# Another form of seven products, another choice of engines in the planner, and norms scaled two token tiles at a time

## The chip, the core and the metric

The kernel runs on one core of a Trainium2 chip. The metric is device time in microseconds (us) of one execution. The engines are TensorE (PE; PEld is its loading of weights), VectorE (DVE), ScalarE (ACT), GpSimd (POOL) and SyncE (SP), which issues every DMA here. All data are float32.

## What is computed

`x` is (64, 256, 128): 64 graphs of 256 nodes with 128 features; all share one adjacency matrix `adj` (256, 256). Four layers follow one another, each `x = layernorm(x + f(x))` over the 128 features.

- Layer 0, five steps of a gated unit. With `m = adj @ h`: `u3 = h @ u3_w.T`; `z = sigmoid([m, m] @ w3_w.T + u3)`; `r = sigmoid([m, m] @ w4_w.T + u3)`; `hv = tanh([m, m] @ w5_w.T + (r * h) @ u5_w.T)`; `h = (1 - z) * h + z * hv`, with biases.
- Layer 1: `h0 = x @ W[0]`, `h1 = x @ W[1]`, `A = softmax` of a masked edge vector; `diag(A) * h0 + offdiag(A) @ h1 + bias`.
- Layer 2: attention over the graph (`softmax` of leaky sums of two scores, masked by `adj`), a layer norm and relu, an aggregation with `adj`, a product with `W1`, a norm and relu, a product with `W2`, relu.
- Layer 3: `adj` is applied up to three times and every power has its own 128 x 128 weight; the sum of these products.

## The kernel before, in words

The 64 graphs are handled as 32 pairs. A pair's `x` is one tile of 128 partitions by 512 columns: four token tiles of 128 features each (two graphs by two halves of the nodes). Matmul operands and results are 512 columns too, so a result fills one PSUM bank; there are eight banks.

**The planner.** The program does not issue operations as it goes through the layers. Every operation is added to a `Schedule` (L119) with its possible engines and a duration for each (`ways`), and what it reads and writes. `order` (L150) then goes through the operations that are ready and always takes the one with the best key: the time at which it could start (plus, where there is a choice of engines, its duration and `SPARE`), and then how late its pair is (`DUE` us from pair to pair, `LAST_DUE` for the last `LAST` pairs, less the work that remains in the pair, plus `HOLD` of its layer). So 32 pairs in different layers are mixed. The order found is written out as it stands; each engine takes its own instructions in that order, and semaphores keep data right. `MARGIN` stretches the planned durations of all engines but PE, `LAG` and `SEEN` are the planned delay until another engine sees a result. `USES` (L44) says that POOL's operations and those of the class "DVE+" (DVE, operands in SBUF alone) exclude each other on a shared resource called PORT. `CLASSES` (L40) gives the number of tiles of each class: X for `x`, T for the transposed input, A for everything of 512 columns, B for 1024, H for layer 2's projected rows, PS for PSUM banks. An operation whose tile class has no free tile is not ready.

**Spreading over the graph.** `spread` (L533) computes `adj @ h` of a pair with four matmuls of 256 columns. `spread7` (L544) does the same with seven products of 128 columns in place of eight, in the manner of Strassen and Winograd: sums of blocks of `h` are made first (`add`, L557, on DVE or POOL), products go to four 128-column blocks X, Y, V, Z of one bank, and results are put together from them by `plus` (L566, DVE) and `copy` (L569 on ACT, L570 on DVE). Four differences of blocks of `adj` are made once (L464). `layer0` (L671) takes `spread7` for pairs from `FIRST` to `n_pairs - FINAL - 1`, else `spread` and an evacuation (`to_sbuf`, L497; `evacuate`, L229, on ACT at L231 or on DVE at L232). A float32 matmul stands in the trace as two instructions.

**Turning.** `turn` (L505) transposes the four 128 x 128 blocks of a tile. For most pairs that is a DVE transpose of 32 x 32 blocks (L520), one DMA to DRAM (L522) and four DMAs back (L528); for the last pairs (`BY_DMA` of them, for each place) it is PE transposes (L514) and an evacuation.

**Norms.** `stats` (L590) and `scale_stats` (L627) find a variance per token; POOL computes its power of -0.5 (L607, L651). `normalize` (L612) then does four token tiles on ACT (L620) or DVE (L615). `scale_tokens` (L654) scales by the token's factor: on ACT one instruction per token tile (L662), on DVE one for all (L664). Layer 1 and layer 2 call it for four token tiles by `scale_norm`, layer 3 for two token tiles of each of two banks.

In the first microseconds four warm-up matmuls run on a constant (L291), `adj`, the first two `x` and the weights arrive, and DVE prepares derived weights. The end is layer 3 of the last pairs (products L822, L823 and L830, statistics, scaling and the store of the result, L836).

Of the kernel before, what the change touches and what calls it, by code (L numbers as in the profile page):

```python
# [8 lines left out]
AF = mybir.ActivationFunctionType  # L9
ALU = mybir.AluOpType  # L10
AX = mybir.AxisListType

P = 128
N = 256
D = 128
STEPS = 5

BY_DMA = {"h": 0, "y": 2, "x1": 3, "x2": 2, "w": 3, "z": 1, "x3": 2}

WARM = 4  # L20


FAST = (0, 1, 2, 3, 4)
FIRST, FINAL = 0, 3

TURN, TT = 0.44, 0.61
LN_EPS = 1e-5
# [9 lines left out]
ROWS = ["l1_bias", "bp", "b1", "gat_g", "gat_b", "b2"]  # L37


CLASSES = {"X": (512, 15), "T": (512, 3), "A": (512, 34), "H": (520, 4), "B": (1024, 6), "S": (32, 64), "PS": (512, 8), "D": (512, 4), "E": (1024, 8)}  # L40

SEEN = {"PE": 0.23, "ACT": 0.16, "DVE": 0.16, "POOL": 0.12, "SP": 0.0}

USES = {"DVE+": ("DVE", "PORT"), "POOL": ("POOL", "PORT")}  # L44

AGAIN = {"DVE": 0.12, "POOL": 0.12}

SPARE = {"DVE": 0.0, "DVE+": 0.0, "POOL": 0.0}


DUE, LAST_DUE, LAST = 20.0, 9.0, 8

MARGIN, LAG = 1.03, 0.8

HOLD = (0.0, -20.0, 0.0, 80.0)


def mm(cols):
# [35 lines left out]
class Op:  # L94
    def __init__(self, pair, ways, reads, writes, number, dma):
        self.pair, self.ways, self.reads, self.writes, self.number, self.dma = pair, ways, reads, writes, number, dma
        self.seen = LAG + (sum(dma) if dma else SEEN[ways[0][0].rstrip("+")])
        self.before, self.then, self.waits, self.ready, self.rest = {}, [], 0, 0.0, 0.0


class Schedule:
# [29 lines left out]
    def order(self, tiles):  # L131
# [6 lines left out]
        for op in reversed(self.ops):  # L138
            us = min(w[1] for w in op.ways) + op.seen
# [6 lines left out]
        while ready:  # L146
            best = None
            for op in ready:
                held = 0.0
                for v in op.holds:  # L150
                    if v.cls and v.ap is None:
                        held = max(held, min((t for t, a in free[v.cls] if full.get(id(a)) or not v.seeded), default=1e9))
                if held == 1e9:
                    continue
                for engine, us, fn in op.ways:
                    us = us if engine == "PE" else us * MARGIN
                    start = max(op.ready, held, *(engines[e] for e in USES.get(engine, (engine,))))
                    late = self.due(op.pair) - op.rest + HOLD[op.layer] if op.pair >= 0 else -1e4
                    key = (start + (us + SPARE.get(engine, 0.0) if len(op.ways) > 1 else 0.0), late, op.number)
                    if best is None or key < best[0]:  # L160
                        best = key, start, op, engine, us, fn
            if best is None:
                raise RuntimeError("no operation can start: too few tiles")
            _, start, op, engine, us, fn = best
# [6 lines left out]
            end = start + us  # L171
# [11 lines left out]
                    full[id(v.ap)] = v.full or v.seeded  # L183
            for x in op.then:
                x.waits -= 1
                same = engine != "SP" and x.ways[0][0].rstrip("+") == engine.rstrip("+")
                x.ready = max(x.ready, end + (AGAIN.get(engine.rstrip("+"), 0.0) if same else op.seen))
                if not x.waits:
                    ready.append(x)

# [7 lines left out]
def kernel(ctx: ExitStack, tc: tile.TileContext, x, xT, adj, adjT, mats, cols, rows, out):  # L198
    nc = tc.nc
# [5 lines left out]
    S = Schedule(n_pairs)  # L205
# [10 lines left out]
    def dve(us, fn, r, w):  # L216
        S.add([("DVE", us, fn)], r, w)
# [18 lines left out]
    aT, a = fixed([2, N], "aT"), fixed([2, N], "a")  # L236
# [224 lines left out]

    aTt = fixed([4, P], "aTt")
    blk_a = lambda j, i: aT.ap[:, j, i * P:(i + 1) * P]
    for k, (p_, q_) in enumerate(((lambda: blk_a(0, 1), lambda: blk_a(0, 0)), (lambda: blk_a(1, 1), lambda: aTt.ap[:, 0, :]),  # L464
                                  (lambda: blk_a(1, 1), lambda: blk_a(0, 1)), (lambda: blk_a(1, 0), lambda: aTt.ap[:, 1, :]))):
        dve(0.25, lambda k=k, p_=p_, q_=q_: nc.vector.tensor_sub(aTt.ap[:, k, :], p_(), q_()), [aT, aTt], [aTt])
    centre(vx, lambda: vx.ap, 2)
    centre(vq, lambda: vq.ap, 2)

# [1 line left out]
    def bank():  # L471

        t = Value("PS", name="ps")
        t.full = True
        return t
# [18 lines left out]
    def tokens(v):  # L494
        return v.at(4, D)
# [48 lines left out]
    def spread7(h, right, terms):  # L544


        sv, t, o = Value("A", name="sums"), bank(), Value("A", name="mT")
        p1, p2, p3, p4 = (Part(sv) for _ in range(4))
        X, Y, Z, V = (Part(t) for _ in range(4))
        o1, o2, o3 = (Part(o) for _ in range(3))  # L550
# [4 lines left out]
        s1, s2, s3, s4 = (lambda k=k: blk(sv, k) for k in range(4))  # L555

        def add(o, x, y, op, r, w):  # L557
            fn = lambda e: e.tensor_tensor(o(), x(), y(), op=op)  # L558
            S.add([("DVE+", 0.2, lambda: fn(nc.vector)), ("POOL", 0.42, lambda: fn(nc.gpsimd))], r, w)

        def product(k, left, rt, r, w, start=False):
            pe(mm(128), lambda: nc.tensor.matmul(blk(t, k), left(), rt(), start=start, stop=True, skip_group_check=True),  # L562
               [*r, right, terms], w)

        def plus(to, k, other, r, w, n=1):
            dve(0.065 + 0.135 * n, lambda: nc.vector.tensor_add(to(), t.at(4, P)[:, k:k + n, :], other()), r, w)  # L566

        def copy(to, k, r, w):
            S.add([("ACT", 0.18, lambda: nc.scalar.copy(to(), blk(t, k))),  # L569
                   ("DVE", 0.2, lambda: nc.vector.tensor_copy(to(), blk(t, k)))], r, w)  # L570
# [12 lines left out]
        plus(lambda: blk(sv, 0), 2, lambda: blk(sv, 1), [V, p2], [p1])  # L583
        product(2, s4, B(1, 1), [p4, V], [V])
        plus(lambda: blk(o, 3), 3, lambda: blk(sv, 0), [Z, p1, o3], [o])
        product(3, H(1, 1), T(3), [h, Z], [Z])
        plus(lambda: o.at(4, P)[:, 1:3, :], 2, lambda: blk(sv, 1)[:, None, :].to_broadcast([P, 2, P]), [V, Z, p2], [o], 2)
        return o

    def stats(y, eps=None):  # L590
# [19 lines left out]
        return s, rs, nmr  # L610

    def normalize(y, o, s, rs, nmr):  # L612
        def by_dve():
            for c in range(4):
                nc.vector.tensor_scalar(tokens(o)[:, c, :], tokens(y)[:, c, :], rs()[:, c:c + 1], nmr()[:, c:c + 1],  # L615
                                        op0=ALU.mult, op1=ALU.add)

        def by_act():
            for c in range(4):
                nc.scalar.activation(tokens(o)[:, c, :], tokens(y)[:, c, :], AF.Identity, bias=nmr()[:, c:c + 1],  # L620
                                     scale=rs()[:, c:c + 1])
# [32 lines left out]
    def scale_tokens(v, o, tiles, s, rs):  # L654

        n, step = len(tiles), tiles[1] - tiles[0]
        ot = lambda: tokens(o)[:, tiles[0]::step, :]
        by = lambda: rs()[:, tiles[0]::step].unsqueeze(2).to_broadcast([P, n, D])

        def by_act():  # L660
            for k, c in enumerate(tiles):
                nc.scalar.mul(tokens(o)[:, c, :], v.at(n, D)[:, k, :], rs()[:, c:c + 1])  # L662
        ways = [("ACT", 0.315 * n, by_act),
                ("DVE" if v.cls == "PS" else "DVE+", 0.135 * n + 0.07, lambda: nc.vector.tensor_mul(ot(), v.at(n, D), by()))]  # L664
        if v.cls != "PS":
            ways.append(("POOL", 0.3 * n + 0.07, lambda: nc.gpsimd.tensor_mul(ot(), v.at(n, D), by())))
# [230 lines left out]
```

## Time and profile before

| what | value |
|---|---|
| median of three runs | 1525.11 us (1524.67 to 1527.51) |
| the profiled execution, its own time | 1524.61 us |
| its span, first to last instruction | 1522.8 us |
| granted TensorE clock | 0.999 |
| PE, PEld busy | 1502.2, 1063.2 us |
| DVE busy | 1296.3 us |
| ACT busy | 936.2 us |
| POOL busy | 562.4 us |
| DMA | 213.86 MB, mean 140 GB/s |

The page of the profile gives busy time by engine, the chain of work that ended last, and groups of instructions with the mean duration of one. Answers of the trace give the same by stage, by line and by who waited for whom. A line is that of the source; where a helper records operations, its line stands for many places, for example L566 for all additions of `spread7`. A busy PE is not a PE at its peak: matmuls are pipelined, so the spacing of their starts says more than their lengths.

### The profile page before, as it was taken

How to read it: one execution, taken by the hardware profiler on the slowest of the kernel's cores; microseconds unless marked ns; L12 is line 12 of the kernel's file. 1: busy time of each engine (PE TensorE's matmuls, PEld its weight loads, DVE VectorE, ACT ScalarE, POOL GpSimd, SP SyncE). 2: the span in 40 equal slices, each digit the busy share in tenths (PEclk: the TensorE clock that was granted, in tenths of full speed). 3: DMA queues.
4: the chain of work that ended last, by engine and by line, in shares of the span. 5: the costliest groups of instructions: out<-in, count | busy, mean ns of one | idle time of the engine just before them, and what ended most of it. 6: DMA issues, size and time to landing. Idle time of an engine off the chain costs nothing.

```text
span 1522.8 us, 26241 instructions
## 1 busy us (share of the span) xinstructions
PE 1502.2 (99%) x7190; PEld 1063.2 (70%) x7190; DVE 1296.3 (85%) x3443; ACT 936.2 (61%) x2805; POOL 562.4 (37%) x784
## 2 busy tenths in 40 slices
PE   9999999999999999999999999999999999999998
PEld 6565656666666677677666776766767666788997
DVE  8988888888989898888998888899888788889763
ACT  2444445666776666656757567677657566768763
POOL 4322223243435433433443344334434132245542
PEclk9999999999999999999999999999999999999999
DMA  7544456576868788686696796767975877776441
GB/s 220 113 97 82 93 117 125 125 159 122 170 132 164 155 169 171 136 164 137 140 177 128 162 185 138 152 134 173 167 147 128 169 133 153 149 149 139 106 89 49
DMA packets 933874, 213.86 MB, mean 140 GB/s; under 512 B 715616, under 2 KB 929248, under 8 KB 933728
## 3 DMA queue, kind: packets, MB, share of 16 engines
q1 hardware_dynamic: 933728, 212.19, 68.6%
q8 instruction: 58, 0.95, 0.3%
q14 instruction: 88, 0.72, 0.2%
HBM read 115.55 MB, written 96.53 MB: 139 GB/s over the span
## 4 chain that ended last, share of the span: by engine, by line
PE 90%; DVE 6%; issue 1%; SPq 1%; DMA 1%; ACT 0%; POOL 0%; POOLq 0%; DVEq 0%; ACTq 0%
PE ps L562 14%; PE ps L539 12%; PE ps L694 8%; PE ps L695 8%; PE ps L687 8%; PE ps L679 8%; PE ps L680 8%; PE ps L716 7%; PE ps L786 4%; PE ps L830 3%; PE ps L822 3%; PE ps L823 3%; PE ps L746 2%; DVE a L566 1%; SPq L528 1%
## 5 line engine op out<-in xcount | busy, mean ns | idle before, releaser
L566 DVE TENSOR_TENSOR a<-ps,a 128x128 f32<-128x128 f32 (+1 forms) x580 | 174.5, 313 | 89.8 <-PE ps L562 75.4
L562 PEld LDWEIGHTS ps<-aTt,a 128*128 128x128 f32 x1102 | 160.9, 192 | 60.1 <-issue 42.4
L683 ACT ACTIVATE a<-ps,bzrh 128x512 f32<-128x512 f32 x160 | 109.8, 686 | 138.3 <-PE ps L680 118.2
L697 ACT ACTIVATE a<-ps,bzrh 128x512 f32<-128x512 f32 x160 | 109.9, 687 | 130.3 <-PE ps L695 126.4
L562 PE MATMUL ps<-aTt,a 128*128 128x128 f32 x1102 | 180.0, 278 | 4.8 <-ACT a L569 3.7
L558 POOL TENSOR_TENSOR a<-a 128x128 f32<-128x128 f32 x138 | 81.8, 606 | 236.2 <-DMA a<-e 112.1
L694 PE MATMUL ps<-a,w 128*128 128x512 f32 x320 | 163.8, 594 | 0.2 <-DVE h L748 0.2
L695 PE MATMUL ps<-a,u5h 128*128 128x512 f32 x320 | 163.5, 592 | 0.2 <-DVE a L685 0.2
L680 PE MATMUL ps<-a,w 128*128 128x512 f32 x320 | 163.4, 592 | 0.0
L687 PE MATMUL ps<-a,w 128*128 128x512 f32 x320 | 162.5, 593 | 0.0
L520 DVE STREAM_TRANSPOSE a<-a 128x512 f32<-128x512 f32 x218 | 152.0, 700 | 3.1 <-ACT a L662 0.4
L562 PEld LDWEIGHTS ps<-aT,a 128*128 128x128 f32 x754 | 118.2, 191 | 52.1 <-issue 34.9
L689 ACT ACTIVATE a<-ps,bzrh 128x512 f32<-128x512 f32 x160 | 109.7, 687 | 68.1 <-PE ps L687 61.5
L716 PEld LDWEIGHTS ps<-W,a 128*128 128x128 f32 x1024 | 131.0, 192 | 26.1 <-issue 22.2
L569 ACT COPY a<-ps 128x128 f32<-128x128 f32 x265 | 66.3, 266 | 129.7 <-PE ps L562 81.1
L562 PE MATMUL ps<-aT,a 128*128 128x128 f32 x754 | 136.7, 278 | 5.5 <-DVE a L566 3.4
L651 POOL TENSOR_TENSOR s<-s,neg_half 128x4 f32<-128x4 f32 x128 | 136.9, 1070 | 9.9
L716 PE MATMUL ps<-W,a 128*128 128x128 f32 x1024 | 136.5, 275 | 0.1
L679 PE MATMUL ps<-a,W 128*128 128x512 f32 x256 | 130.9, 593 | 0.0
L231 ACT COPY a<-ps 128x512 f32<-128x512 f32 (+1 forms) x162 | 82.6, 513 | 73.8 <-PE ps L539 36.7
L643 ACT ACTIVATE a<-ps 128x128 f32<-128x128 f32 x428 | 112.5, 282 | 23.1 <-PE ps L716 8.6
L648 POOL TENSOR_SCALAR s<-s 128x4 f32<-128x4 f32 x96 | 29.0, 302 | 249.2 <-ACT a L643 218.9
(197 smaller groups left out, 3302.2 us busy)
## 6 DMA issues: line engine op xcount, KB each, us to landing
e<-a SPq DMA_DIRECT2D x278, 256.0 KB
a<-e SPq DMA_DIRECT2D x1112, 64.0 KB
e<-b SPq DMA_DIRECT2D x29, 512.0 KB
b<-e SPq DMA_DIRECT2D x116, 128.0 KB
x<-x_in SPq DMA_DIRECT2D x32, 256.0 KB
t<-xT_in SPq DMA_DIRECT2D x32, 256.0 KB
a<-d SPq DMA_DIRECT2D x32, 256.0 KB
y_out<-a SPq DMA_DIRECT2D x32, 256.0 KB
```

What stands on the lines that cost most here:

```text
L520: dve(n / 512 * 0.55 + 0.09, lambda: nc.vector.transpose(st.at(n), i.at(n)), [i], [st])
L539: nc.tensor.matmul(t.at(2, N)[:, b, :], tokens(i)[:, 2 * b + j, :], right.ap[:, j, :], start=(b == j == 0), stop=(j == 1), skip_group_chec ...
L562: pe(mm(128), lambda: nc.tensor.matmul(blk(t, k), left(), rt(), start=start, stop=True, skip_group_check=True), [*r, right, terms], w)
L566: dve(0.065 + 0.135 * n, lambda: nc.vector.tensor_add(to(), t.at(4, P)[:, k:k + n, :], other()), r, w)
L643: nc.scalar.activation(tokens(junk)[:, c, :], v.at(len(tiles), D)[:, k, :], AF.Square, scale=D ** -0.5, accum_out=mv()[:, c, 1:2])
L651: pool(1.02, lambda: nc.gpsimd.tensor_tensor(rs(), rs(), neg_half.ap, op=ALU.pow), [s, neg_half], [s])
L679: nc.tensor.matmul(t.at(512), mat("u3"), hT.at(512), start=True, stop=False)
L680: nc.tensor.matmul(t.at(512), w4.ap, mT.at(512), start=False, stop=True)
L687: pe(mm(512), lambda t=t, mT=mT: nc.tensor.matmul(t.at(512), w3.ap, mT.at(512), start=False, stop=True, skip_group_check=True), [w3, mT, t ...
L694: nc.tensor.matmul(t.at(512), w5.ap, mT.at(512), start=True, stop=False)
L695: nc.tensor.matmul(t.at(512), u5h.ap, r.at(512), start=False, stop=True)
L716: nc.tensor.matmul(tokens(t)[:, c, :], tokens(i)[:, c, :], w(), start=(first and k == c == 0), stop=(k == len(lefts) - 1), skip_group_chec ...
```

## The change

The diff has these parts.

- Constants of the planner: `FIRST, FINAL` from 0, 3 to 2, 2 (pairs 2 to 29 use `spread7` instead of 0 to 28); `BY_DMA` of z from 1 to 2 and of x3 from 2 to 0; numbers of tiles; `SPARE`, `DUE`, `MARGIN`, `HOLD`.
- A class "POOL-" for POOL operations that do not occupy PORT. The helper `pool` uses it (short operations on 4 elements, among them the power).
- `order` first picks for each operation the way that ends first, `SPARE` included, and compares operations by start time and lateness afterwards.
- `spread7`: three sums (one of them of 256 columns), seven products to three blocks, four copies (ACT or DVE) and three additions of 128 columns. Before, it had four sums, two copies, three additions of 128 and one of 256 columns.
- `normalize` and `scale_norm` are two operations of two token tiles each; each chooses its engine.

```diff
-BY_DMA = {"h": 0, "y": 2, "x1": 3, "x2": 2, "w": 3, "z": 1, "x3": 2}
+BY_DMA = {"h": 0, "y": 2, "x1": 3, "x2": 2, "w": 3, "z": 2, "x3": 0}
-FIRST, FINAL = 0, 3
+FIRST, FINAL = 2, 2
-CLASSES = {"X": (512, 15), "T": (512, 3), "A": (512, 34), "H": (520, 4), "B": (1024, 6), "S": (32, 64), "PS": (512, 8), "D": (512, 4), "E": (1024, 8)}
+CLASSES = {"X": (512, 14), "T": (512, 4), "A": (512, 30), "H": (520, 5), "B": (1024, 5), "S": (32, 64), "PS": (512, 8), "D": (512, 4), "E": (1024, 8)}
-USES = {"DVE+": ("DVE", "PORT"), "POOL": ("POOL", "PORT")}
+USES = {"DVE+": ("DVE", "PORT"), "POOL": ("POOL", "PORT"), "POOL-": ("POOL",)}
-SPARE = {"DVE": 0.0, "DVE+": 0.0, "POOL": 0.0}
-DUE, LAST_DUE, LAST = 20.0, 9.0, 8
-MARGIN, LAG = 1.03, 0.8
-HOLD = (0.0, -20.0, 0.0, 80.0)
+SPARE = {"DVE": 0.6, "DVE+": 1.0, "POOL": 0.4}
+DUE, LAST_DUE, LAST = 30.0, 9.0, 8
+MARGIN, LAG = 1.06, 0.8
+HOLD = (0.0, -40.0, 0.0, 60.0)
...
+                way = None
                 for engine, us, fn in op.ways:
                     us = us if engine == "PE" else us * MARGIN
                     start = max(op.ready, held, *(engines[e] for e in USES.get(engine, (engine,))))
-                    late = self.due(op.pair) - op.rest + HOLD[op.layer] if op.pair >= 0 else -1e4
-                    key = (start + (us + SPARE.get(engine, 0.0) if len(op.ways) > 1 else 0.0), late, op.number)
-                    if best is None or key < best[0]:
-                        best = key, start, op, engine, us, fn
+                    end = start + us + SPARE.get(engine, 0.0)
+                    if way is None or end < way[0]:
+                        way = end, start, op, engine, us, fn
+                late = self.due(op.pair) - op.rest + HOLD[op.layer] if op.pair >= 0 else -1e4
+                key = (way[1], late, op.number)
+                if best is None or key < best[0]:
+                    best = key, *way[1:]
...
     def pool(us, fn, r, w):
-        S.add([("POOL", us, fn)], r, w)
+        S.add([("POOL-", us, fn)], r, w)
...
     def spread7(h, right, terms):
-        sv, t, o = Value("A", name="sums"), bank(), Value("A", name="mT")
+        sv, t, o = Value("A", name="sums"), Value("PS", name="ps"), Value("A", name="mT")
...
-        product(0, H(0, 0), B(0, 0), [h], [X, Y, Z, V], start=True)
-        copy(lambda: blk(o, 3), 0, [X], [o3])
-        add(s1, H(1, 0), H(1, 1), ALU.add, [h], [p1])
-        add(s2, s1, H(0, 0), ALU.subtract, [h, p1], [p2])
-        add(s3, H(0, 0), H(1, 0), ALU.subtract, [h], [p3])
-        add(s4, H(0, 1), s2, ALU.subtract, [h, p2], [p4])
-        product(0, H(0, 1), B(1, 0), [h, X], [X])
-        copy(lambda: blk(o, 0), 0, [X], [o])
-        product(1, s2, T(1), [p2, Y], [Y])
-        plus(lambda: blk(sv, 1), 1, lambda: blk(o, 3), [Y, o3], [p2])
-        product(2, s1, T(0), [p1, V], [V])
-        product(3, s3, T(2), [p3, Z], [Z])
-        plus(lambda: blk(sv, 0), 2, lambda: blk(sv, 1), [V, p2], [p1])
-        product(2, s4, B(1, 1), [p4, V], [V])
-        plus(lambda: blk(o, 3), 3, lambda: blk(sv, 0), [Z, p1, o3], [o])
-        product(3, H(1, 1), T(3), [h, Z], [Z])
-        plus(lambda: o.at(4, P)[:, 1:3, :], 2, lambda: blk(sv, 1)[:, None, :].to_broadcast([P, 2, P]), [V, Z, p2], [o], 2)
+        def sum_(us, us_pool, fn, r, w):
+            S.add([("DVE+", us, lambda: fn(nc.vector)), ("POOL", us_pool, lambda: fn(nc.gpsimd))], r, w)
+        def plus(to, k, r, w):
+            dve(0.2, lambda: nc.vector.tensor_add(blk(o, to), blk(t, k), blk(o, to)), r, w)
+        product(0, H(0, 0), B(0, 0), [h], [X, Y, V], start=True)
+        sum_(0.335, 0.8, lambda e: e.tensor_sub(sv.at(4, P)[:, 0:2], h.at(4, P)[:, 0::2], h.at(4, P)[:, 2:4]), [h], [p1])
+        sum_(0.2, 0.46, lambda e: e.tensor_sub(s2(), s1(), H(0, 0)()), [h, p1], [p2])
+        sum_(0.2, 0.46, lambda e: e.tensor_add(s4(), s2(), H(0, 1)()), [h, p2], [p4])
+        copy(0, 0, [X], [o0])
+        product(1, s1, T(0), [p1, V], [V])
+        copy(3, 1, [V], [o3])
+        product(2, H(0, 1), B(1, 0), [h, Y], [Y])
+        plus(0, 2, [Y, o0], [o, o0])
+        product(0, s2, T(1), [p2, X], [X])
+        copy(1, 0, [X], [o1])
+        product(1, s4, B(1, 1), [p4, V], [V])
+        plus(1, 1, [V, o1], [o, o1])
+        product(0, s3, T(2), [p1, X], [X])
+        plus(3, 0, [X, o3], [o, o3])
+        product(0, H(1, 1), T(3), [h, X], [X])
+        copy(2, 0, [X], [o])
...
     def normalize(y, o, s, rs, nmr):
+        for half in ((0, 1), (2, 3)):
...
-        S.add([("ACT", 1.56, by_act), ("DVE" if y.cls == "PS" else "DVE+", 1.04, by_dve)], [y, s], [o])
+            S.add([("ACT", 0.78, by_act), ("DVE" if y.cls == "PS" else "DVE+", 0.52, by_dve)], [y, s], [o])
...
     def scale_norm(y, o, eps=None):
-        scale_tokens(y, o, range(4), *scale_stats([(y, range(4))], eps))
+        s, rs = scale_stats([(y, range(4))], eps)
+        for first in (0, 2):
+            scale_tokens(y, o, range(first, first + 2), s, rs, first)
```

The differences of blocks of `adj` (L464) are formed with other signs, with as many instructions.

More of the change, by code (lines that the diff above doesn't have):

```diff
@@ L96, in __init__ @@
         self.pair, self.ways, self.reads, self.writes, self.number, self.dma = pair, ways, reads, writes, number, dma
-        self.seen = LAG + (sum(dma) if dma else SEEN[ways[0][0].rstrip("+")])
+        self.seen = LAG + (sum(dma) if dma else SEEN[ways[0][0].rstrip("+-")])
         self.before, self.then, self.waits, self.ready, self.rest = {}, [], 0, 0.0, 0.0
@@ L185, in order @@
                 x.waits -= 1
-                same = engine != "SP" and x.ways[0][0].rstrip("+") == engine.rstrip("+")
-                x.ready = max(x.ready, end + (AGAIN.get(engine.rstrip("+"), 0.0) if same else op.seen))
+                same = engine != "SP" and x.ways[0][0].rstrip("+-") == engine.rstrip("+-")
+                x.ready = max(x.ready, end + (AGAIN.get(engine.rstrip("+-"), 0.0) if same else op.seen))
                 if not x.waits:
@@ L463 @@
     blk_a = lambda j, i: aT.ap[:, j, i * P:(i + 1) * P]
-    for k, (p_, q_) in enumerate(((lambda: blk_a(0, 1), lambda: blk_a(0, 0)), (lambda: blk_a(1, 1), lambda: aTt.ap[:, 0, :]),
-                                  (lambda: blk_a(1, 1), lambda: blk_a(0, 1)), (lambda: blk_a(1, 0), lambda: aTt.ap[:, 1, :]))):
-        dve(0.25, lambda k=k, p_=p_, q_=q_: nc.vector.tensor_sub(aTt.ap[:, k, :], p_(), q_()), [aT, aTt], [aTt])
+    dve(0.25, lambda: nc.vector.tensor_sub(aTt.ap[:, 0, :], blk_a(0, 1), blk_a(0, 0)), [aT], [aTt])
+    for k, other in ((1, lambda: aTt.ap[:, 0, :]), (2, lambda: blk_a(0, 1))):
+        dve(0.25, lambda k=k, other=other: nc.vector.scalar_tensor_tensor(aTt.ap[:, k, :], blk_a(1, 1), -1.0, other(),
+                                                                         op0=ALU.mult, op1=ALU.subtract), [aT, aTt], [aTt])
+    dve(0.25, lambda: nc.vector.tensor_add(aTt.ap[:, 3, :], aTt.ap[:, 1, :], blk_a(1, 0)), [aT, aTt], [aTt])
     centre(vx, lambda: vx.ap, 2)
@@ L544, in spread7 @@
     def spread7(h, right, terms):
-        sv, t, o = Value("A", name="sums"), bank(), Value("A", name="mT")
-        p1, p2, p3, p4 = (Part(sv) for _ in range(4))
-        X, Y, Z, V = (Part(t) for _ in range(4))
-        o1, o2, o3 = (Part(o) for _ in range(3))
+        sv, t, o = Value("A", name="sums"), Value("PS", name="ps"), Value("A", name="mT")
+        p1, p2, p4 = (Part(sv) for _ in range(3))
+        X, Y, V = (Part(t) for _ in range(3))
+        o0, o1, o3 = (Part(o) for _ in range(3))
         blk = lambda v, k, n=1: v.at(512)[:, k * P:(k + n) * P]
@@ L554, in spread7 @@
         T = lambda k: lambda: terms.ap[:, k, :]
[L555 to L559, printed above, removed]
+        s3, s1, s2, s4 = (lambda k=k: blk(sv, k) for k in range(4))
         def product(k, left, rt, r, w, start=False):
@@ L563, in product @@
                [*r, right, terms], w)
-        def plus(to, k, other, r, w, n=1):
-            dve(0.065 + 0.135 * n, lambda: nc.vector.tensor_add(to(), t.at(4, P)[:, k:k + n, :], other()), r, w)
+        def sum_(us, us_pool, fn, r, w):
+            S.add([("DVE+", us, lambda: fn(nc.vector)), ("POOL", us_pool, lambda: fn(nc.gpsimd))], r, w)
         def copy(to, k, r, w):
-            S.add([("ACT", 0.18, lambda: nc.scalar.copy(to(), blk(t, k))),
-                   ("DVE", 0.2, lambda: nc.vector.tensor_copy(to(), blk(t, k)))], r, w)
@@ L581, in spread7 @@
-        product(2, s1, T(0), [p1, V], [V])
-        product(3, s3, T(2), [p3, Z], [Z])
-        plus(lambda: blk(sv, 0), 2, lambda: blk(sv, 1), [V, p2], [p1])
-        product(2, s4, B(1, 1), [p4, V], [V])
-        plus(lambda: blk(o, 3), 3, lambda: blk(sv, 0), [Z, p1, o3], [o])
-        product(3, H(1, 1), T(3), [h, Z], [Z])
-        plus(lambda: o.at(4, P)[:, 1:3, :], 2, lambda: blk(sv, 1)[:, None, :].to_broadcast([P, 2, P]), [V, Z, p2], [o], 2)
+            S.add([("ACT", 0.18, lambda: nc.scalar.copy(blk(o, to), blk(t, k))),
+                   ("DVE", 0.2, lambda: nc.vector.tensor_copy(blk(o, to), blk(t, k)))], r, w)
@@ L612, in normalize, with by_dve, by_act @@
     def normalize(y, o, s, rs, nmr):
[L613 to L621, printed above, removed]
-        S.add([("ACT", 1.56, by_act), ("DVE" if y.cls == "PS" else "DVE+", 1.04, by_dve)], [y, s], [o])
+        for half in ((0, 1), (2, 3)):
+            def by_dve(half=half):
+                for c in half:
+                    nc.vector.tensor_scalar(tokens(o)[:, c, :], tokens(y)[:, c, :], rs()[:, c:c + 1], nmr()[:, c:c + 1],
+                                            op0=ALU.mult, op1=ALU.add)
+            def by_act(half=half):
+                for c in half:
+                    nc.scalar.activation(tokens(o)[:, c, :], tokens(y)[:, c, :], AF.Identity, bias=nmr()[:, c:c + 1],
+                                         scale=rs()[:, c:c + 1])
+            S.add([("ACT", 0.78, by_act), ("DVE" if y.cls == "PS" else "DVE+", 0.52, by_dve)], [y, s], [o])
     def layer_norm(y, o):
@@ L652, in scale_stats, with scale_tokens @@
         return s, rs
-    def scale_tokens(v, o, tiles, s, rs):
+    def scale_tokens(v, o, tiles, s, rs, first=0):
         n, step = len(tiles), tiles[1] - tiles[0]
-        ot = lambda: tokens(o)[:, tiles[0]::step, :]
-        by = lambda: rs()[:, tiles[0]::step].unsqueeze(2).to_broadcast([P, n, D])
+        vt = lambda: v.at(first + n, D)[:, first:, :]
+        ot = lambda: tokens(o)[:, tiles[0]:tiles[-1] + 1:step, :]
+        by = lambda: rs()[:, tiles[0]:tiles[-1] + 1:step].unsqueeze(2).to_broadcast([P, n, D])
         def by_act():
             for k, c in enumerate(tiles):
-                nc.scalar.mul(tokens(o)[:, c, :], v.at(n, D)[:, k, :], rs()[:, c:c + 1])
+                nc.scalar.mul(tokens(o)[:, c, :], vt()[:, k, :], rs()[:, c:c + 1])
         ways = [("ACT", 0.315 * n, by_act),
-                ("DVE" if v.cls == "PS" else "DVE+", 0.135 * n + 0.07, lambda: nc.vector.tensor_mul(ot(), v.at(n, D), by()))]
+                ("DVE" if v.cls == "PS" else "DVE+", 0.135 * n + 0.07, lambda: nc.vector.tensor_mul(ot(), vt(), by()))]
         if v.cls != "PS":
-            ways.append(("POOL", 0.3 * n + 0.07, lambda: nc.gpsimd.tensor_mul(ot(), v.at(n, D), by())))
+            ways.append(("POOL", 0.3 * n + 0.07, lambda: nc.gpsimd.tensor_mul(ot(), vt(), by())))
         S.add(ways, [v, s], [o])
     def scale_norm(y, o, eps=None):
-        scale_tokens(y, o, range(4), *scale_stats([(y, range(4))], eps))
+        s, rs = scale_stats([(y, range(4))], eps)
+        for first in (0, 2):
+            scale_tokens(y, o, range(first, first + 2), s, rs, first)
     def layer0(x0, hT):
```

## The prediction

> **What bounds the kernel.** I read the page's first part, then the chain of waits, then busy time by stage, and last who waits for whom. The page says TensorE (PE) is busy 99% and carries 90% of the chain that ended last:
>
> ```profile
> PE 1502.2 (99%) x7190; PEld 1063.2 (70%) x7190; DVE 1296.3 (85%) x3443; ACT 936.2 (61%) x2805; POOL 562.4 (37%) x784
> ...
> PE 90%; DVE 6%; issue 1%; SPq 1%; DMA 1%; ACT 0%; POOL 0%; POOLq 0%; DVEq 0%; ACTq 0%
> ```
>
> Ends of matmuls are modelled, so I take the spacing of their starts instead. The chain of waits gives it for each shape (start, length, line, number of instructions):
>
> ```profile
> 147.62 1.56 PE ps L562 x14
> 155.86 1.72 PE ps L687 x4
> 216.31 1.73 PE ps L539 x8
> 232.11 1.78 PE ps L716 x16
> ```
>
> So an instruction of 128 columns takes 0.112 us, of 256 columns 0.216, of 512 columns 0.430. Counts by shape in the trace: 3822 of 128 or 130 columns, 1656 of 256, 1600 of 512, 64 transposes of 0.109, and about 8 us in the prologue: 428 + 358 + 688 + 7 + 8 = 1489 us. Before the first matmul lie 1.2 us, from the start of the last to the end of the span 6.6. 1522.8 - 1489 - 7.8 = 26 us in which PE stands between matmuls. That is all that anything but less PE work can win. 22 of the 26 us stand at products of L562, the seven-product code.
>
> The Trainium skill's page Perfetto Trace Analysis, section Identifying the Most-Contended Engine, would judge PE by its weight loads' busy share; at 70% that would leave some 450 us to win (an estimate from that rule). The spacings above do not bear this out, and the sum does not use it.
>
> Busy time by stage (columns: length, then busy us and count of PE, PEld, DVE, ACT, POOL):
>
> ```profile
> 0.00:38.00 38.00, 34.33 (x161) 24.27 (x162) 33.56 (x97) 11.32 (x26) 17.96 (x36) 1.00 0.79 220
> ...
> 190.00:380.00 190.00, 187.09 (x838) 119.07 (x837) 165.65 (x429) 107.80 (x298) 63.90 (x93) 1.00 0.64 130
> 380.00:570.00 190.00, 187.50 (x945) 133.54 (x944) 168.77 (x449) 130.98 (x404) 80.02 (x108) 1.00 0.80 158
> ...
> 1140.00:1330.00 190.00, 190.00 (x831) 132.15 (x830) 158.52 (x390) 122.22 (x350) 53.42 (x68) 1.00 0.72 146
> 1330.00:1500.00 170.00, 170.00 (x973) 150.27 (x972) 128.79 (x411) 118.05 (x416) 77.67 (x106) 1.00 0.57 116
> ```
>
> By spacing, the stalls are 5.9 us before 38, 20.6 from 190 to 1140, and nothing from 1140 on. Where they are, DVE is busy 87 to 89%. The waits say the same (engine and line, releaser: us, times, longest):
>
> ```profile
> DVE a L566 <- PE ps L562: 75.4, 91, 2.3
> ACT a L569 <- PE ps L562: 81.1, 90, 5.7
> ...
> PE ps L562 <- ACT a L569: 5.0, 11, 1.4
> PE ps L562 <- DVE a L566: 4.9, 12, 1.1
> ```
>
> The 580 additions of L566 found DVE idle and waiting for the product 91 times, one in six; the 265 copies of L569 found ACT so one time in three. DVE has the backlog.
>
> **The change, part by part.**
>
> PE work. Pairs with seven products go from 29 (0 to 28) to 28 (2 to 29): five spreads more in full, each 8 x 0.216 = 1.73 against 14 x 0.112 = 1.57: +0.8 us. Transposes on PE: one more for z, two fewer for x3, each 4 x 0.109: -0.4. Sum +0.4 us. The new form has seven products too.
>
> Waits in the new form. A product that overwrites or adds to a block must wait for its reader. Before: one such wait behind a copy and two behind DVE additions, 3 x 145 = 435. After: H11T3 waits behind a DVE addition, s2T1, s3T2 and s4B11 behind copies: 4 x 140 = 560. Each is free if PE has other work for the round trip; uncovered ones cost about 0.5 us (the longest repeated stalls behind L569 are 0.52). At the present rate per wait, 9 us behind DVE become 9 x 140/290 = 4.3, 4.2 behind ACT outside the prologue become 4.2 x 420/145 = 12.2: +3.3 us. This is the change's own cost.
>
> Relief of DVE. Additions: 174.5 us become 420 x 0.273 = 115: -60. Sums (L558): 271 of 580 are on DVE, 84 us; the new form has 140 of 256 columns and 280 of 128, and with SPARE the cheapest way is mostly POOL (0.49 + 0.4 against 0.21 + 1.0): I take one in five on DVE, about 27 us, -57; ends -84 and +52. Scaling, mean squares and evacuations, which SPARE 0.6 pushes to ACT: L664 50.7, L637 and L639 29.9, L232 22, L615 7; half to two thirds go: -61, ends 0 and -110. DVE falls by about 178 to 1120 us, 73%; ends 1290 and 1040. ACT takes the copies (560 x 0.25 x 0.9 = 126 against 66: +60) and these (four scalings of 0.294 for one of DVE): +88, so about 1084 us, 71%. The split of a scaling into two operations costs one dispatch and lets the halves begin on either engine; on DVE a 512-wide one takes 669 ns and a 256-wide one 412, so 0.15 us each, off the path.
>
> The shared port. The plan before kept POOL and DVE's SBUF operations from overlapping, the short POOL operations too. The trace says for DVE sums of 128 columns: 280 ns with nothing on POOL, 281 beside a 4-element POOL operation, 714 beside a POOL tensor operation. L651 and L607 hold POOL 208 us; the new class "POOL-" gives that time to DVE in the plan, and the rows say that it is free.
>
> ```profile
> L558 POOL TENSOR_TENSOR a<-a x138: 446/458/1011, 38.9 to 1252.5; 128x128 f32<-128x128 f32 x138
> L558 DVE TENSOR_TENSOR a<-a,a x124: 245/282/1354, 57.8 to 1216.8; 128x128 f32<-128x128 f32 x124
> ```
>
> The skill's GPSIMD Engine Reference, Key points, speaks against more sums on POOL: it shares SBUF interfaces with DVE and is about half as fast for elementwise work. The rows say 458 against 282, and 714 for a DVE sum that collides. [...]
>
> What is it worth? The 20.6 us between 190 and 1140 lie between gone and doubled. More room in the plan (port, DVE, MARGIN 1.06) makes operands ready earlier and lets other pairs' work cover the round trips. The nearest row is the stage 1140 to 1330: DVE 83%, 92 products, no stall; but it has a third of the products. I take a fall by 40% net of the +3.3: **-8 us**; ends -20 and +21.
>
> Prologue. Now PE waits there for the seven-product round trips and DVE's set-up work:
>
> ```profile
> 10.31 0.46 PE L562 MATMUL ps<-aT,a 128*128 128x128 f32 x2 [1.36 <-ACT a L569]
> ...
> 12.54 0.49 PE L562 MATMUL ps<-aTt,a 128*128 128x128 f32 x2 [0.35 <-ACT a L569]
> ...
> 14.60 1.02 PE L679 MATMUL ps<-t,W 128*128 128x512 f32 x2
> ```
>
> With plain spreads for pairs 0 and 1 (x is there at 4.7 and 5.7) both are done at 8.3, and L680 needs only an evacuation of about 0.6: the first L679 can come at 8 to 9 instead of 14.6. The loads and single-pair latency remain: I take **-2 us**, ends -5 and 0.
>
> Tail. x3 of the last two pairs now goes through DRAM. A turn in the loaded middle took 11.1 us (571.3 to 582.4):
>
> ```profile
> 571.26 0.71 DVE a L520
> ...
> 572.88 2.97 DMA e<-a
> ...
> 580.15 2.22 DMA a<-e
> ```
>
> The last x3 is ready at 1500.9 and its products L822 started at 1511.0, behind products of other pairs. By DMA it would be there at 1512: 0 to +1.5 us; I take 0, since the tail moves fewer bytes (46 GB/s). If HOLD 60 for 80 leaves less layer-3 work as cover, it costs up to the 11 less the 1.7 of the PE way: +9.
>
> DUE 30 for 20 brings fewer pairs into flight, as do the tiles (X 14, A 30); nothing in the trace prices it: 0, ends as for the stalls above. Banks of the new form no longer count as full for seeded tiles; eight banks rotate, 0.
>
> Sum: 1524.6 (this execution: span 1522.8 and 1.8 around it) + 0.4 - 8 - 2 = 1515.0; the median of the runs is 0.5 above this execution: **1515.5 us**, own range 1504 to 1522.
>
> **Rivals.**
>
> Nothing gained: the relief falls where nothing waits, and the added waits eat what the ports give; or the plan leaves the sums on DVE. For it: PE is already at 98%. Against: stalls sit where DVE is fullest. -2 + 0.4: 1523.5.
>
> Slower: ACT's round trips. Three copies in a row now release PE, behind an in-order ACT of 71% that also has runs of four scalings (1.65 us, L620). If one wait in seven of 560 stays uncovered by 0.47 us, 37 us for 20.6: +16, about 1540. It decides from one in eleven (25 us of stalls in all after 38). Against: ACT now answers at once one time in three.
>
> Slower: too few pairs in flight or a bare tail, +9 for the tail: 1533. Against: the tail now has 9.6 us of other pairs' products in hand.
>
> **How the numbers follow.** Forecast 0.55, nothing gained 0.16, ACT's round trips 0.20, flight or tail 0.09. Measurement can tell about 0.2% (3 us) from no change. Faster by more 0.56, within 0.15, slower 0.29. The range 1504 to 1540 leaves out the best of the first and the worse half of the slower cases.
>
> **What would show it.** DVE at 1040 to 1200 us, ACT at 1030 to 1130; 1960 product instructions; the first L679 before 10 us; PE idle from 190 to 1140 below 8 us (10.8 now); no PE gap in the last 40 us. Wrong if waits of PE for the copies' line exceed 12 us, if DVE stays over 1250, or if PE idles after 1140.

## The result, and the profile after

The changed kernel takes 1515.2 us (median; 1514.48 to 1515.56) against 1525.1 before; the ratio is 0.9931, 95% interval 0.9914 to 0.9948. Its profiled execution has a span of 1513.6 us. The page of the changed kernel, busy time and the chain that ended last:

```profile
PE 1498.1 (99%) x7156; PEld 1060.8 (70%) x7156; DVE 1191.8 (79%) x3102; ACT 1006.1 (66%) x3173; POOL 626.9 (41%) x835
...
PE 94%; DVE 3%; ACT 1%; DMA 1%; issue 1%; SPq 0%; POOLq 0%; ACTq 0%; POOL 0%; DVEq 0%
```

DVE lost 104 us, ACT gained 70, POOL 64. DVE's part of the chain went from 6% to 3%. Busy time by stage of the changed kernel (length, then busy us and count of PE, PEld, DVE, ACT, POOL):

```profile
0.00:38.00 38.00, 36.35 (x177) 26.66 (x178) 28.79 (x84) 14.59 (x37) 20.78 (x39) 1.00 0.69 195
38.00:190.00 152.00, 151.26 (x564) 88.77 (x563) 106.16 (x218) 69.15 (x152) 33.09 (x47) 1.00 0.48 102
190.00:380.00 190.00, 189.28 (x905) 128.01 (x904) 166.07 (x427) 136.68 (x434) 83.32 (x109) 1.00 0.74 152
380.00:570.00 190.00, 188.21 (x935) 134.50 (x934) 163.72 (x426) 134.15 (x443) 94.26 (x121) 1.00 0.77 161
...
1330.00:1490.00 160.00, 158.47 (x910) 138.50 (x909) 124.60 (x415) 131.71 (x470) 74.52 (x97) 1.00 0.66 138
```

By these rows PE now stands 0.7 us between 190 and 380 us where it stood 2.9; between 1330 and 1490 it stands 1.5 where it stood nothing until 1500. By the spacing of matmul starts, as in the prediction, the span before is 1488.9 of PE work, 7.8 at both ends and 26.2 of stalls; after, 1489.2, 7.7 and 16.7. From here on "stall" is this difference. It went from 5.9 to 2.1 us before 38, from 20.1 to 11.8 between 38 and 1330, and from 0.1 to 2.9 after 1330.

Who waits for whom in the changed kernel (engine and line, releaser: us, times, longest). L565 is the product, L572 the copy on ACT, L576 the addition on DVE, L545 the plain spread:

```profile
DVE a L576 <- PE ps L565: 84.9, 86, 5.8
...
ACT a L572 <- PE ps L565: 70.1, 97, 3.0
```

DVE now sits idle until the product comes one time in five (86 of 420; it was 91 of 580), ACT likewise (97 of 489; it was 90 of 265). In this the two queues have become alike. What PE itself waits for:

```profile
PE ps L565 <- DVE a L576: 3.9, 9, 1.2
PE ps L295 <- DVE ones L293: 1.2, 1, 1.2
PE ps L545 <- DMA a<-e: 1.2, 1, 1.2
PE ps L565 <- ACT a L572: 1.0, 3, 0.6
```

There are 420 products behind a copy where there were 145 (of the 560 copies 489 ran on ACT), and yet PE's idle time behind the ACT copies fell from 5.0 us to 1.0. The start, PE alone in order of time (start, length, line):

```profile
4.84 4.94 PE L545 MATMUL ps<-aT,x 128*128 128x256 f32 x16
9.62 1.02 PE L690 MATMUL ps<-t,W 128*128 128x512 f32 x2
10.48 1.02 PE L691 MATMUL ps<-a,w 128*128 128x512 f32 x2
```

Two plain spreads stand where the seven products of two pairs stood, and the gates' first product starts at 9.62 instead of 14.60.

### The profile page after: what moved, and what is told of

It reads as the page before. It is cut to its first block, busy times and chain, and to the rows that moved or that the text cites. A ratio compares the mean times of both kernels' runs of the same rounds, so it can differ in the third digit from the quotient of the medians.

```text
span 1513.6 us, 26330 instructions
## 1 busy us (share of the span) xinstructions
PE 1498.1 (99%) x7156; PEld 1060.8 (70%) x7156; DVE 1191.8 (79%) x3102; ACT 1006.1 (66%) x3173; POOL 626.9 (41%) x835
## 4 chain that ended last, share of the span: by engine, by line
PE 94%; DVE 3%; ACT 1%; DMA 1%; issue 1%; SPq 0%; POOLq 0%; ACTq 0%; POOL 0%; DVEq 0%
PE ps L565 14%; PE ps L545 13%; PE ps L705 9%; PE ps L706 9%; PE ps L698 9%; PE ps L690 9%; PE ps L691 9%; PE ps L727 7%; PE ps L841 4%; PE ps L834 3%; PE ps L797 3%; PE ps L833 3%; PE ps L757 2%; DVE b L772 1%; DVE a L576 0%
## 5 line engine op out<-in xcount | busy, mean ns | idle before, releaser
L565 PEld LDWEIGHTS ps<-aTt,a 128*128 128x128 f32 x1064 | 165.5, 191 | 82.5 <-issue 56.3
L579 POOL TENSOR_TENSOR a<-a 128x256 f32<-128x256 f32 x100 | 83.0, 830 | 296.8 <-DMA a<-e 102.7
L576 DVE TENSOR_TENSOR a<-ps,a 128x128 f32<-128x128 f32 x420 | 109.6, 280 | 106.0 <-PE ps L565 84.9
L565 PE MATMUL ps<-aTt,a 128*128 128x128 f32 x1064 | 186.6, 276 | 5.1 <-DVE a L576 3.9
L572 ACT COPY a<-ps 128x128 f32<-128x128 f32 x489 | 117.4, 272 | 88.9 <-PE ps L565 70.1
L651 ACT ACTIVATE a<-ps 128x128 f32<-128x128 f32 x456 | 121.1, 287 | 48.2 <-PE ps L727 23.8
L659 POOL TENSOR_TENSOR s<-s,neg_half 128x4 f32<-128x4 f32 x128 | 144.4, 1128 | 9.3
L727 PE MATMUL ps<-W,a 128*128 128x128 f32 x1024 | 141.8, 275 | 0.0
L565 PEld LDWEIGHTS ps<-aT,a 128*128 128x128 f32 x728 | 108.4, 191 | 26.4 <-issue 20.8
L565 PE MATMUL ps<-aT,a 128*128 128x128 f32 x728 | 125.7, 276 | 0.6 <-issue 0.2
```

Of the source, the lines that this page charges most:

```text
L572: S.add([("ACT", 0.18, lambda: nc.scalar.copy(blk(o, to), blk(t, k))), ("DVE", 0.2, lambda: nc.vector.tensor_copy(blk(o, to), blk(t, k)))] ...
L651: nc.scalar.activation(tokens(junk)[:, c, :], v.at(len(tiles), D)[:, k, :], AF.Square, scale=D ** -0.5, accum_out=mv()[:, c, 1:2])
L727: nc.tensor.matmul(tokens(t)[:, c, :], tokens(i)[:, c, :], w(), start=(first and k == c == 0), stop=(k == len(lefts) - 1), skip_group_chec ...
```

## The experiments

The first theory was the prediction's: **relief**, room on DVE and on the shared port. Its rivals were **form** (the new products wait less by themselves) and **planning** (the gain belongs to one order among many). All runs are in this table; "b" kernels start from the kernel before, "a" kernels from the changed one. Stalls and DVE's busy time are from each one's profiled execution; that of a_copies_dve, 1541.3 us, is the slowest of its four (the others 1535 to 1537).

| kernel | median us | ratio to before (95%) | stalls to 38 | 38 to 1330 | from 1330 | DVE us |
|---|---|---|---|---|---|---|
| before | 1525.1 | | 5.9 | 20.1 | 0.1 | 1296 |
| b_null | 1552.3 | 1.0175 (1.0158 to 1.0192) | 6.1 | 30.6 | 18.6 | 1296 |
| b_null2 | 1557.4 | 1.0210 (1.0195 to 1.0226) | 6.5 | 26.0 | 25.7 | 1303 |
| b_null_x16 | 1539.8 | 1.0098 (1.0083 to 1.0114) | 6.0 | 15.5 | 20.4 | 1286 |
| b_new_form | 1549.8 | 1.0160 (1.0145 to 1.0175) | 6.8 | 22.6 | 20.0 | 1284 |
| b_choice | 1530.7 | 1.0035 (1.0022 to 1.0048) | 9.4 | 15.7 | 8.5 | 1209 |
| b_pool_free | 1531.9 | 1.0040 (1.0029 to 1.0051) | 5.0 | 22.4 | 8.5 | 1309 |
| changed | 1515.2 | 0.9931 (0.9914 to 0.9948) | 2.1 | 11.8 | 2.9 | 1192 |
| a_null | 1518.3 | 0.9955 (0.9940 to 0.9970) | 0.9 | 15.4 | 2.0 | 1185 |
| a_null2 | 1518.1 | 0.9955 (0.9940 to 0.9970) | 0.8 | 15.2 | 1.8 | 1182 |
| a_norm4 | 1522.5 | 0.9982 (0.9972 to 0.9991) | 0.9 | 14.0 | 6.8 | 1184 |
| a_old_form | 1533.1 | 1.0051 (1.0036 to 1.0066) | 1.4 | 23.6 | 9.7 | 1209 |
| a_pairs | 1541.9 | 1.0110 (1.0095 to 1.0125) | 6.4 | 33.8 | 4.5 | 1186 |
| a_copies_dve | 1536.6 | 1.0071 (1.0054 to 1.0088) | 1.5 | 34.9 | 6.2 | 1258 |

**Changes without meaning.** These were meant as controls and turned out to say the most.

```diff
 a_null
-MARGIN, LAG = 1.06, 0.8
+MARGIN, LAG = 1.061, 0.8
 a_null2
-MARGIN, LAG = 1.06, 0.8
+MARGIN, LAG = 1.059, 0.8
 b_null
-MARGIN, LAG = 1.03, 0.8
+MARGIN, LAG = 1.031, 0.8
 b_null2
-MARGIN, LAG = 1.03, 0.8
+MARGIN, LAG = 1.029, 0.8
```

> The changed kernel with MARGIN 1.061 for 1.060, a change without meaning that only makes the planner order some operations otherwise. Relief theory (the gain of 8 us of stalls comes from room on DVE and on the shared port): within 2 us of the changed kernel, 1513 to 1517. Planning theory (the gain is one lucky order among many): several us off, 1518 or more, or 1511 or less. It also measures how far any other edit can be read.

> The kernel before with MARGIN 1.031 for 1.030, a change without meaning that only makes the planner order some operations otherwise. Relief and form theories: within 2 us of 1525. Planning theory: several us off either way, and single edits of 2 to 3 us cannot be read from one run.

> The kernel before with MARGIN 1.029 for 1.030, the change without meaning the other way. Theory of a rare good order (the constants of before happen to give one): again 1535 or more, with the last x after 1260. Rival (1.031 was one bad order among good ones): 1523 to 1530.

> The changed kernel with MARGIN 1.059 for 1.060. If the changed kernel's orders are steady by themselves: 1513 to 1520, as with 1.061 (1518.3). If that was chance: 1525 or more.

One part in a thousand of the planned durations costs the kernel before 27 and 32 us, and the changed kernel 3. Planning had b_null and b_null2 right, and a_null (1518.3) by a hair; relief's "within 2 us" missed; a_null2 came out steady, as the expectation had it if 1518 was no chance. So the order of the kernel before was a good one beside these two, and its 1525 us are not what its form and constants give as a rule; the changed kernel came out at 1515 to 1518 three times. Three orders on each side are few, but they do not overlap. What an idle edit cost the kernel before is mostly its end (18.5 of some 29 us of stalls in b_null, 25.6 of 32 in b_null2). The end of b_null, PE alone in order of time:

```profile
1523.80 1.11 PE L514 MATMUL ps<-ident,a 128*128 128x128 f32 x4 [3.48 <-DVE a L664]
1526.91 2.08 PE L716 MATMUL ps<-W,a 128*128 128x128 f32 x8 [2.00 <-ACT ps L231]
1533.03 3.78 PE L539 MATMUL ps<-aT,x 128*128 128x256 f32 x8 [4.04 <-DVE x L615]
```

The last pair walks through its norms, turns and products alone, and PE waits for each. In b_null the last tanh of layer 0 ran at 1430.6, before at 1380.2: the last pair's layers 1 to 3 came 50 us later, with little other work left beside them. In the changed kernel and both idle edits of it, stalls after 1330 are 2.9 us or less. The loads of x differ too: in the changed kernel they come one every 44 to 50 us for a long stretch (648, 697, 741, 787, 836, 886, 934), though later also as a clump and a gap (997 twice, then 1112); in the kernel before they come in clumps (720 and 721, 822 and 838, 1166 and 1167). The last x is issued at 1236 before, at 1230 in the changed kernel, at 1295 in b_null and 1302 in b_null2. Regular loads alone do not keep PE busy: a_pairs below loads x as evenly (674, 720, 767, 813, 862, 914, 957) and is slow.

**Is the late tile the cause?** One x tile more for b_null:

```diff
 b_null_x16 (on top of b_null)
-CLASSES = {"X": (512, 15), ...
+CLASSES = {"X": (512, 16), ...
```

> The kernel before with MARGIN 1.031 and 16 tiles for x instead of 15. With MARGIN 1.031 alone the last x was loaded at 1295 us (1236 before), and 257 us passed from there to the end with 19 us of stalls after 1330. Late-tile theory (the last pair waits for an x tile, and its own chain then sets the end): with one tile more the last x is loaded by 1240, the stalls after 1330 fall below 8 us, time 1525 to 1540. Rival (the stalls are spread over the order, the tile is not the cause): 1545 to 1555 again.

The time, 1539.8, lies just inside what the late-tile theory expected, but by luck, for both its signs failed: the last x came at 1265, not by 1240, and the stalls after 1330 stayed at 20.4. The 12 us gained lie in the middle (30.6 to 15.5). All six b kernels load their last x later (1265 to 1302) and have a longer end than the kernel before, but the two do not go in step: with 1265 the end has 20.4 us of stalls, with 1267 (b_choice) and 1275 (b_pool_free) 8.5. What makes the last pair late is not shown.

This run says one thing more. Its middle, 15.5, is that of the changed kernel's idle edits (15.4 and 15.2), with the old form, the old choice of engines and 1286 us on DVE. So an order with hardly any relief can have a middle like theirs.

**The form of seven products, put in alone and taken out alone** (`spread7` and the differences of `adj` blocks, which belong together):

```diff
 b_new_form: spread7 and aTt of the changed kernel in the kernel before
 a_old_form: spread7 and aTt of the kernel before in the changed kernel
```

> The kernel before with the new form of seven products alone. Form theory: most of the gain after the prologue, 1517 to 1519. Relief theory: a part of it, since only the additions leave DVE (about 50 us): 1521 to 1524. Round trips (four waits per set for three, at the rate of before +3 us): 1526 to 1530.

> The changed kernel with the form of seven products of before (four sums, two copies, three additions of 128 columns and one of 256). Relief theory: DVE gets back some 60 us of additions and part of the sums, so DVE about 1260 us busy and half of the gain lost, about 1519. Form theory (the new products wait less by themselves): all of the gain after the prologue lost, 1521 or more. Planning theory: within 2 us of 1515.

Alone it wins nothing, and at 1550 us all three theories missed it: 22.6 us of stalls in the middle, inside the span of the kernel before and its idle edits (20.1 to 30.6). Taken out, stalls in the middle double, from 11.8 to 23.6, though DVE has only 17 us more to do (1209; relief expected 1260). What PE waits for in a_old_form (L566 the product, L570 the addition on DVE):

```profile
PE ps L566 <- DVE a L570: 8.1, 15, 1.3
PE ps L830 <- DMA a<-e: 5.7, 2, 5.0
PE ps L566 <- ACT a L573: 3.2, 8, 0.7
```

The old form's products stand behind DVE's additions again, 8.1 us for 3.9. The 5.7 us behind a DMA are at its end. At 1533 relief's 1519 and planning's 1515 missed; form's "1521 or more" was met, though 6.8 us of the loss are stalls at the end. As form failed on the other side, this does not decide for it.

**The choice of engines, and the port, put in alone:**

```diff
 b_choice: order picks the way that ends first; key = (way[1], late, op.number)
-SPARE = {"DVE": 0.0, "DVE+": 0.0, "POOL": 0.0}
+SPARE = {"DVE": 0.6, "DVE+": 1.0, "POOL": 0.4}
 b_pool_free: "POOL-": ("POOL",) added to USES
     def pool(us, fn, r, w):
-        S.add([("POOL", us, fn)], r, w)
+        S.add([("POOL-", us, fn)], r, w)
```

> The kernel before with the new choice of engines alone (the way that ends first with SPARE 0.6, 1.0 and 0.4; operations then compared by start and lateness). Relief theory: DVE falls by 60 to 100 us, time 1518 to 1522. Form theory: no change, 1523 to 1527.

> The kernel before with the class for short POOL operations that do not occupy the shared port, alone. Relief theory: 208 us of port time come free in the plan, 1521 to 1524. Rivals: no change, 1523 to 1527.

In time both are 6 to 7 us slower than before, so every expected time missed; beside the idle edits of the kernel before they are 20 us faster. By stage they differ. b_choice takes 87 us from DVE, as relief had it, and its stalls in the middle are 15.7, below the kernel before and its two idle edits, but no lower than the 15.5 of b_null_x16, which took only 10 us from DVE; the start (9.4) and the end (8.5) take the gain back. b_pool_free leaves the middle where it was and DVE's work too.

The page's first part of b_choice:

```profile
PE 1504.1 (98%) x7190; PEld 1066.5 (70%) x7190; DVE 1208.9 (79%) x3153; ACT 944.3 (62%) x2824; POOL 752.1 (49%) x1090
```

What left DVE went to POOL, 752 us for 562, not to ACT.

**DVE filled again:**

```diff
 a_copies_dve
-            S.add([("ACT", 0.18, lambda: nc.scalar.copy(blk(o, to), blk(t, k))),
-                   ("DVE", 0.2, lambda: nc.vector.tensor_copy(blk(o, to), blk(t, k)))], r, w)
+            S.add([("DVE", 0.2, lambda: nc.vector.tensor_copy(blk(o, to), blk(t, k)))], r, w)
```

> The changed kernel with the four copies of each set of seven products on DVE alone, never on ACT: 490 copies of 0.28 us move, DVE from 1192 to about 1310 us busy, ACT from 1006 to about 890. Relief theory: stalls after the prologue back to 20 us or more, 1521 to 1530. Form or planning theory: DVE's fill does not matter by itself, 1513 to 1518.

DVE rose by 66 us, not 118, since the planner moved other work away. Stalls in the middle went from 11.8 to 34.9 and the time to 1536.6, more than relief expected (20 us or more, 1530 at most), and PE waits for DVE by name (L575 the addition, L572 the copy, here on DVE):

```profile
PE ps L565 <- DVE a L575: 12.2, 17, 2.2
PE ps L565 <- DVE a L572: 2.8, 7, 0.5
```

This is the run that speaks most clearly for relief: the same form, the same constants, and the waits behind the additions are three times as long (12.2 for 3.9). It does not show it, for the next run has nearly as long waits there without any more work on DVE.

**The first pairs:**

```diff
 a_pairs
-FIRST, FINAL = 2, 2
+FIRST, FINAL = 0, 3
```

> The changed kernel with seven products for pairs 0 to 28 again (FIRST 0, FINAL 3). Prologue theory (plain spreads for the first two pairs save 2 us of stalls and pairs 0 and 1 cost 0.8 us of PE work in sum): stalls before 38 us back to about 6, time +1.5 to +2, about 1517. Rival: the prologue's gain came from the new form's order and stays: 1515 or less.

The start did what the prologue theory expected, 2.1 to 6.4 us of stalls, and the table agrees: every kernel with seven products for the first pairs has 5.0 to 9.4 us there, every one with plain spreads 0.8 to 2.1. The time, 1542 against 1517, missed: the middle went to 33.8, with DVE at 1186 us, and relief has no answer to that. What PE waits for in a_pairs:

```profile
PE ps L565 <- DVE a L576: 10.2, 18, 1.2
PE ps L727 <- DMA a<-e: 1.8, 1, 1.8
PE ps L565 <- ACT a L572: 1.8, 4, 0.7
```

The additions on DVE again. Most of it lies between 190 and 570:

```profile
190.00:380.00 190.00, 180.29 (x842) 119.88 (x841) 151.54 (x390) 124.92 (x395) 72.69 (x97) 0.99 0.66 136
380.00:570.00 190.00, 183.14 (x876) 128.05 (x875) 156.87 (x417) 133.80 (x425) 85.76 (x115) 1.00 0.79 163
```

Here PE stands 9.7 and 6.9 us with DVE busy 80 and 83%; in the changed kernel it stands 0.7 and 1.8 us in these stages with DVE busy 87 and 86%. So PE can wait for DVE's additions where DVE is less full, and a full DVE need not make it wait: how full DVE is does not by itself set these stalls. Whether they come from the two pairs as such or only from another order is open; the run shows that the changed kernel is steady against an idle edit of MARGIN, not against every edit.

**Halves of the norms:**

```diff
 a_norm4 (normalize likewise)
-        for first in (0, 2):
-            scale_tokens(y, o, range(first, first + 2), s, rs, first)
+        scale_tokens(y, o, range(4), s, rs)
```

> The changed kernel with every norm scaled by one operation of four token tiles again. Theory of halves (a half fits between urgent copies on ACT, a run of four scalings of 1.65 us holds them up): stalls between 38 and 1330 rise by 4 us or more, 1519 to 1530. Rival (no effect beyond that of an idle change of the order): 1513 to 1520. The split as such saves no work, on DVE it adds 0.15 us for each norm.

Against the changed kernel 7 us slower, against its idle edits 4; the middle (14.0) is where theirs is, and the end has 4 to 5 us more. The time is in the range of the theory of halves, but its sign, 4 us or more in the middle, did not come (2.2 against the changed kernel, a fall of 1 against the idle edits), so that halves let urgent copies through on ACT is not borne out; that the halves help the end is a reading of one order.

No run was faster than the changed kernel.

## Why the prediction came out right, point by point

- **PE's floor.** Right: 1489.2 us of PE work and 7.7 at the ends, so only stalls were to be won. PE work was forecast at +0.4 and is +0.3.
- **Prologue**, -2 us: the stalls fell by 3.8, inside its ends of -5 and 0, and a_pairs brings them back (6.4). The first gate product came at 9.62, forecast 8 to 9. This step is shown, by the undoing and by the table.
- **The stalls in the middle**, -8 us: -8.3 between 38 and 1330. The size was a choice between ends (a fall by 40%), and that it hit is in good part luck: it was net of 3.3 us for new waits that did not come and counted on a relief of DVE of 178 us, of which 104 came. That the relief made the fall is not shown (below).
- **Tail**, 0: +2.8. It was mis-sized, and PE idle after 1140 was one of the prediction's own signs of being wrong. The largest piece is not x3: PE stood 1.2 us from 1363.7 for a turn of h in layer 0 of a late pair (L545 reads it with `aT`); the other pieces are 0.5 us and less by spacing. The chain of waits of the changed kernel there (start, length, what):

```profile
1356.15 2.43 DMA e<-a
...
1360.45 4.37 DMA a<-e
...
1364.91 1.97 PE ps L545 x8
```

- **The waits of the new form**, +3.3 us: the term that failed. It took a fixed rate per wait. Where 145 products behind a copy left PE idle 5.0 us behind ACT, 420 left it 1.0. So the number of waits does not set their cost; what does was not measured. The term also began from 4.2 us behind ACT outside the prologue, where the view of waits has 3.3 (5.0 less 1.7 before 38); with these it would have been about +1.6.
- **Relief of DVE**, -178 us: -104. Additions gave 65 (60 forecast), sums 65 (57 forecast: 41 of the 420 stayed on DVE, one in ten for one in five). The scaling, mean squares and evacuations, forecast at -61, gave only 4: scaling 51.3 us on DVE where it had 50.5, mean squares 19.3 for 30.0, evacuations 17.7 for 21.6, normalize 16.0 for 6.6. What is left of the -104, some +30, is other work of DVE that grew; 12 of it are copies that ran on DVE (19.6 for 7.1). ACT got 70 us, of which the copies are 51, and not 148; its 1006 us lie below the 1030 that the prediction gave as a sign.
- **The shared port.** That the short POOL operations cost DVE nothing is what the rows said (281 ns beside one, 280 alone); freeing the port in the plan alone (b_pool_free) left the middle among the orders of the kernel before (22.4 in 20.1 to 30.6).
- **Fewer pairs in flight**, priced at 0: no loss shows, but DUE and HOLD were not tried by themselves.
- **What the prediction lacked.** It took 1525 us as the mark of the kernel before. Two idle edits put this kernel at 1552 and 1557, and none of the six b kernels landed within 5 us of 1525 (1531 to 1557). So a change that only reshuffles it can cost some 30 us, and the rival "nothing gained" at 1523.5 was less likely than it looked. The number was right because the new parts and constants together gave an order nearly as well covered at the end as the old one (2.8 us worse) and 12 us better before it; the prediction has no step that says why the end held, and there it was lucky.

So, shown: the gain is 9.5 us of stalls, less at the start and in the middle and more at the end. Shown by undoing: the plain spreads of the first pairs carry the start. Not shown: that relief of DVE carries the middle. Without the new form or without the copies on ACT the middle is worse (23.6 and 34.9), but a_pairs makes it as bad (33.8) with no more work on DVE, and b_null_x16 makes it good (15.5) with only 10 us less on DVE than the kernel before, so each of these runs may have measured its order. Not settled: why a_pairs fills the middle with stalls at the same DVE load, what makes the last pair late in the b kernels, and how much each of DUE, HOLD and SPARE carries. Several orders of each edited kernel would tell an edit from its order; they were not run.

## What to carry to other kernels

Where a planner in the program sets the order, change a constant by a thousandth first: the spread of the times it gives is the least that another edit must exceed to mean something (here 27 and 32 us on one kernel, 3 on the other), and a part that is slower alone may still be part of a faster whole. When the main engine is at its floor, count its work by the spacing of starts, and read the rest by stage: start, middle and end moved independently here. The number of added waits is no measure of their cost: 420 left PE idle less than 145 had. And before a stall is put down to a full engine, compare how full that engine is in another run that stalls less there.

## What the runs showed of the hardware

A stall at the end can cost more than its length. In b_null PE stood 3.5, 2.0 and 4.0 us between 1520 and 1533, and the granted clock fell to half (columns as above; the number after POOL's count is the clock):

```profile
1510.00:1520.00 10.00, 8.80 (x44) 6.94 (x44) 5.91 (x22) 2.45 (x5) 2.82 (x4) 1.00 0.05 12
1520.00:1526.00 6.00, 1.43 (x7) 0.84 (x6) 1.86 (x9) 1.02 (x2) 1.25 (x2) 0.61 0.15 44
1526.00:1530.00 4.00, 2.08 (x8) 1.78 (x8) 0.88 (x2) 0.86 (x2) 0.00 (x0) 0.50 0.00 0
1530.00:1536.00 6.00, 2.97 (x7) 2.43 (x8) 2.23 (x13) 0.00 (x0) 1.27 (x2) 0.50 0.00 1
1536.00:1542.00 6.00, 5.33 (x15) 3.95 (x15) 0.00 (x0) 1.17 (x2) 0.00 (x0) 0.51 0.00 0
1542.00:1546.00 4.00, 3.77 (x17) 2.65 (x15) 0.81 (x5) 0.74 (x2) 0.00 (x0) 1.00 0.00 0
```

Eight instructions of 256 columns took 3.78 us there; at full clock, at 703.46 in the kernel before, they took 1.89. By such doubled times about 5 of the 18.6 us of stalls at b_null's end are slow clock (an estimate). The Trainium skill's page TensorE: Matmul & The Clock Gate, section Part 1: The HAM clock gate, has a table of two states, half and full clock, half after at least one idle window of some 3.4 us. The 0.50 here agrees with its half clock; the window is not read from these rows, for the 0.61 puts the fall at about 1521.3 (an estimate), one us into the first of the three stalls. In the kernel before and the changed one the clock was full (0.999 and 1.000 over the span), so the gain owes nothing to it.
